# Batch 0's token scores on VectorE, y behind the first queries, first context blocks by thirds

## The chip, the core and the metric

One core of a Trainium2 chip runs the whole program in one launch. The metric is the device time of one execution in microseconds (us); all operands are float32. The engines are TensorE (PE, its weight loads PEld), VectorE (DVE), ScalarE (ACT), GpSimd (POOL) and SyncE (SP), which here only issues DMAs. Each engine works through its own queue in program order; the order is written out by hand in the source, and semaphores keep the data dependences.

## The reference

The inputs are 16 batches of 100 rows x (640 wide) and a context of 722 rows (384 wide), of which the last T = 4 are "tokens".

```python
query = x @ Wq;  keyt = enc @ Wk;  valt = enc @ Wv       # enc: 718 rows
hs = mha(query, keyt, valt)                              # 8 heads of 80
ca_q1 = einsum('btc,th->bch', ca, Wq_ca)[:, indices, :]  # ca: the 4 tokens
ca_hs1 = mha(ca_q1, x, x)
ca_hs2 = mha(ca_hs1 @ Wq, ca @ Wk_ca, ca @ Wv_ca)
out = (hs + ca_hs2) @ Wout + b_out + x
```

## The kernel before

**Context products.** Keys and values are made by a scheme that replaces the 18 block products of a 3 x 3 by 3 x 2 blocking by 15 products of sums of blocks. The context of a batch is cut into three thirds u of its 718 rows (240 columns each, transposed) and three chunks c of its 384 channels; `enc_sums` (L484) forms 13 sums or differences of these blocks on POOL (L505, 128x240 each), and `weight_sums` (L509) forms 12 differences of weight blocks on DVE (L529): 128x256 for the key weights `wk_sb`, 128x320 for the value weights `wv_sb`. `weight_sums(..., late)` takes the seven that leave the raw blocks alone (False), the five that overwrite them (True), or all. `Values` and `Keys` (L413, L456) go through a plan of 15 products in banks A to E; each product is copied (ACT, L410) or added (DVE, L408) into its place, and a bank cannot be used again before that.

**Start.** Five small matmuls run on zeros (`idle_ps`). Wk arrives transposed, by heads (`packed`, 96 KB each, even heads first, on the SP and ACT queues), and batch 0's context by single blocks (`load_first`, nine DMAs of 120 KB). `first_keys` (L595) turns Wk back on PE (`turn_back`, L587) and multiplies batch 0's keys directly, without the scheme: chunks 0 and 1 of the output with context channels c = 0 first, then three more `turn_back`s, then the rest (L619, 36 products in all). `last_keys` (L635) does the fifth chunk. In the trace one float32 product shows as two matmul records.

Behind it come, on DVE, the weight sums of `wk_sb`; on POOL two memsets and `enc_sums(enc)` of batch 0; on PE the tokens' keys `k_ps` (L1287), and from these, masked by heads on DVE (L1299), the products `m_ps` with Wq transposed (L1311), five of them, each copied by DVE (L1319). Three of the `wv_sb` sums stand on DVE behind each of the last four copies.

**Second attention.** `Second(b)` works out the token path. `keys(m)` (L765) places `m` into `m2` on POOL; `products` (L792) multiplies it with x to `y_ps` (L798) and sums `g` on DVE; `scores1` (L826) makes the 100 x 800 scores `e1` on POOL with four products (L833) and three additions (L840); `softmax1` (L844) finds their maximum by eight DVE steps of `Maximum` (L706) and subtracts it (L850); `exponentials1` (L852) is ACT's; `softmax2` (L855) multiplies by y to `z_ps` (L860).

For batch 0 the order is: `m_ps`, `last_keys`, `y_ps`, all five `queries` (L538), the tokens' values `va_ps`. POOL has batch 0's `scores1`, then `keys` and `enc_sums` for batch 1.

**Batch loop (L1366).** Per batch three groups of `scores` (L645, `s_ps`, copied by ACT at L681 and L687), their running maximum (`larger`, L1394 to L1396, and L1405), `z_ps`, the next batch's `y_ps`, then value products of this batch mixed with key products of the next (`vv.go`, `kk.go`, `both`). Between them stand `subtract` (L1384) and `exponential` (L1392) of the three score tiles, and at the end the products with the values (L1541, L1559). Batch 0 has an order of its own: three value and three key products, and the exponentials of its tokens between them, before `softmax2`. The last batch has no next keys; its value products follow `END_PLAN`, its third score tile is subtracted on POOL behind the first.

Of the kernel before, what the change touches and what calls it, by code (L numbers as in the profile page):

```python
# [10 lines left out]
ALU = mybir.AluOpType  # L11
# [4 lines left out]
NH, D = 8, 80  # L16
CAD, T = 384, 4
SK = 722 - T
P = 128
HC = H // P  # L20
CC = CAD // P

KT = SK // 3 + 1
# [124 lines left out]
def kernel(  # L148
# [144 lines left out]
    def load_first(queue, u, c):  # L293
        queue.dma_start(
            out=a_raw(enc, u, c),
            in_=enct[0][:, c, u * (KT - 1) : u * (KT - 1) + KT],
        )

    for h in range(0, NH, 2):
        (nc.scalar, nc.sync)[h // 2 % 2].dma_start(**packed(wkt_sb, wkt, h))  # L300
    load_first(nc.sync, 0, 0)
    load_first(nc.scalar, 1, 0)
    load_first(nc.sync, 2, 0)
    for h in range(1, NH, 2):
        (nc.scalar, nc.sync)[h // 2 % 2].dma_start(**packed(wkt_sb, wkt, h))
    nc.sync.dma_start(
        out=wkt_sb[:, 4], in_=wkt.rearrange("(h k) n -> h k n", h=NH)[:, 64:]
    )
    for c in range(1, CC):
        for u in range(3):  # L310
            load_first(nc.sync, u, c)
    tokens = pb_tile("tokens")
    beside = wide("beside")[:, : CC * (B * T + P)]
    cat_sb = beside[:, : CC * B * T].rearrange("p (c n) -> p c n", c=CC)
# [2 lines left out]
    nc.sync.dma_start(out=cat_sb, in_=cat.rearrange("p c b t -> p c (b t)"))  # L317
    nc.sync.dma_start(out=wkca_sb, in_=wkca.rearrange("(c p) n -> p c n", p=P))
    wqt_sb = wout_sb
    nc.sync.dma_start(out=wqt_sb, in_=wqt.rearrange("(c p) r -> p c r", p=P))  # L320
    nc.sync.dma_start(
        out=wv_sb[:, : 2 * CC].rearrange("p (c g) n -> p c (g n)", g=2),
        in_=wv.rearrange("(c p) n -> p c n", p=P),
    )
    xT = inp.tile([P, 2, HC, S], F32, tag="xT", name="xT_0", bufs=1)
    nc.sync.dma_start(out=xT, in_=xt[0:2].rearrange("b p c s -> p b c s"))
    halves = [t[:, u] for t in [scores_tile(f"wq_{i}") for i in range(NP)] for u in range(2)]
# [178 lines left out]
            begun = begun or first  # L506
        return begun

    def weight_sums(engine, w, late=None, part=slice(None)):  # L509
# [17 lines left out]
        for f, left, right in sums[part]:  # L527
            if late is None or late == (f in (5, 7, 13, 3, 14)):
                engine.tensor_tensor(at(f), left, right, ALU.subtract)  # L529
# [65 lines left out]
    def first_keys(enc):  # L595

        banks = {}
        copies = nc.scalar.copy, nc.vector.tensor_copy

        def begin(n, get):  # L600
            if get is pair:
                both = pair(f"kT_ps_0_{n}")
                banks[n] = [both[:, k] for k in range(2)]
            else:
                banks[n] = [get(f"kT_ps_0_{n}_{k}") for k in range(2)]

        for n in range(2):
            turn_back(n, nc.vector.tensor_copy)
            begin(n, pair)
        for c, chunks in ((0, (0, 1)), (0, (2, 3)), (1, range(4)), (2, range(4))):  # L610
            if len(banks) < 4 and 2 in chunks:
                for n in (2, 3, 4):
                    turn_back(n, copies[n % 2])
                begin(2, psum1)
                begin(3, psumk)
            for n in chunks:
                for bank, thirds in zip(banks[n], ((0, 1), (2,))):
                    for i, u in enumerate(thirds):
                        nc.tensor.matmul(  # L619
                            bank[:, i * KT : (i + 1) * KT],  # L620
                            wk_sb[:, 2 * c + n % 2, n // 2],
                            a_raw(enc, u, c),
                            start=(i == 0 and c == 0),
                            stop=(c == CC - 1),
                            skip_group_check=True,
                        )
        for n in banks:
            for bank, thirds in zip(banks[n], ((0, 1), (2,))):
                w = len(thirds)
                nc.scalar.copy(  # L630
                    kT[:, n, thirds[0] : thirds[0] + w],
                    bank[:, : w * KT].rearrange("p (u k) -> p u k", u=w),
                )
# [143 lines left out]
    class Second:  # L777
# [45 lines left out]
                ],  # L823
            )

        def scores1(self, behind=None, tokens=range(T)):  # L826
            b, g = self.b, self.g
            e = e1[:S].rearrange("p (h s) -> p h s", h=NH)
            for t in tokens:
                to = e if t == 0 else product_tile(f"e1_{b}_{t}")[:S].rearrange(  # L830
                    "p (h s) -> p h s", h=NH
                )
                first = nc.gpsimd.tensor_tensor(  # L833
                    to,
                    self.ca[:, t, :].unsqueeze(1).to_broadcast([S, NH, S]),
                    g[:, :, t].unsqueeze(2).to_broadcast([S, NH, S]),
                    ALU.mult,
                )
                if t:
                    nc.gpsimd.tensor_tensor(e, e, to, ALU.add)  # L840
                elif behind:
                    wait_for(first, behind)

# [418 lines left out]
    nc.gpsimd.memset(most[96:, :], LOW)  # L1262
    nc.gpsimd.memset(e1[96:, :], LOW)
    weight_sums(nc.vector, wk_sb, False)
    weight_sums(nc.vector, wk_sb, True)
    enc_sums(enc)

# [40 lines left out]
    for c in range(HC):  # L1308
        m_ps = psum(f"m_ps_{c}")
        for n, heads in enumerate(HEADS):  # L1310
            nc.tensor.matmul(  # L1311
                m_ps[:, heads[0] * B * T : (heads[-1] + 1) * B * T],
                wqt_sb[:, n, c * P : (c + 1) * P],
                k2T[n],
                start=(n == 0),
                stop=(n == HC - 1),
                skip_group_check=True,
            )
# [12 lines left out]
    second.copy()  # L1331
    second.scores1()
    keys(load_m(1))
    enc_sums(enc_next)
    tiles = queries_tiles(0)
    for n in range(HC):
        queries(0, xT, tiles, n)

    for e, lo in enumerate((64, 0)):
# [19 lines left out]
                    stop=(cc == CC - 1),  # L1359
                )  # L1360
    nc.scalar.copy(vaT.rearrange("p c n -> p (c n)"), va_ps[:, : HC * B * T])
    second.softmax1()

    xT_at = [None]
    last, late, second_next = None, False, Second(1, xT)
    for b in range(B):  # L1366
# [38 lines left out]
        nc.vector.tensor_tensor(most[:KN], st[0][:, 0], st[0][:, 1], ALU.max)  # L1405
# [24 lines left out]
        if b + 1 < B:  # L1430

            def both(n):
                vv.go(n)
                kk.go(n)
# [61 lines left out]
        else:  # L1496
# [132 lines left out]
```

## Time and profile before

| | us |
|---|---|
| median of 3 runs | 929.56 (929.08 to 931.22) |
| profiled execution | 928.27 |
| its span in the trace | 926.6 |
| PE busy | 913.8 (99%) |
| DVE, POOL, ACT busy | 659.0, 626.3, 376.1 |

The profiled execution's own time is 1.67 us longer than the span of its instructions. Times of the trace count from the start of the span. A row of the timeline merges equal instructions that follow each other: start, busy time, engine, line, operation, tiles, shapes, count, and in square brackets the idle time ahead and what ended it.

### The profile page before, as it was taken

The page shows a single profiled execution, that of the slowest core. Times are in us where ns is not written, and L with a number is a line of the kernel's source. Part 1 is how long each engine was busy: PE and PEld are TensorE (multiplying, and loading weights), DVE is VectorE, ACT ScalarE, POOL GpSimd, SP SyncE. Part 2 cuts the span into 40 slices and gives each one's busy share as a digit, 9 for nine tenths or more (in the row PEclk, how much of TensorE's full clock was granted, in tenths as well). Part 3 has the DMA queues.
Part 4 walks back from the last instruction along what each step waited for, and adds up shares of the span by engine and source line. Part 5 has one row for each costly group of instructions (what it writes and reads, how often), then busy time and mean ns, then how long its engine had stood idle before and what let it go on. Part 6 is the DMA issues. An engine that isn't in the chain of part 4 may idle for free.

```text
span 926.6 us, 26069 instructions
## 1 busy us (share of the span) xinstructions
PE 913.8 (99%) x11151; PEld 777.7 (84%) x11151; DVE 659.0 (71%) x1115; ACT 376.1 (41%) x654; POOL 626.3 (68%) x659
## 2 busy tenths in 40 slices
PE   9998999999999999999999999999999999999998
PEld 8976979888887989888798887988888888888865
DVE  2479796888729786685966759579792887828783
ACT  2343533435425354532434334344541444425351
POOL 9485788576955778477584766846796566955723
PEclk9999999999999999999999999999999999999999
DMA  8603262051401504141141402204140151401331
GB/s 288 211 13 83 64 131 73 6 141 34 109 11 34 141 6 109 44 118 25 40 103 43 131 12 65 78 15 133 43 109 10 34 138 37 110 11 45 86 84 32
DMA packets 68060, 69.50 MB, mean 75 GB/s; under 512 B 25192, under 2 KB 61352, under 8 KB 67944
## 3 DMA queue, kind: packets, MB, share of 16 engines
q1 hardware_dynamic: 67016, 66.97, 26.9%
q8 instruction: 88, 1.44, 0.7%
q10 hardware_dynamic: 464, 0.52, 0.2%
q0 software_dynamic: 464, 0.34, 0.2%
q14 instruction: 28, 0.23, 0.1%
HBM read 62.14 MB, written 8.94 MB: 77 GB/s over the span
## 4 chain that ended last, share of the span: by engine, by line
PE 95%; DVE 3%; issue 1%; ACT 1%; DMA 0%; ACTq 0%; DVEq 0%
PE s_ps L659 12%; PE v_psA L437 11%; PE v_psB L437 9%; PE k_psA L468 8%; PE a_ps L1559 7%; PE q_ps L542 7%; PE k_psB L468 6%; PE kT_ps L566 6%; PE r_ps L1541 4%; PE v_psC L437 4%; PE k_psC L468 3%; PE y_ps L798 2%; PE kT_ps L619 2%; PE o_psy L1127 2%; PE v_psD L437 2%; PE v_psE L437 2%
## 5 line engine op out<-in xcount | busy, mean ns | idle before, releaser
L833 POOL TENSOR_TENSOR e<-ca,g 100x800 f32<-100x800 f32 x64 | 97.8, 1540 | 95.6 <-DVE most L1396 77.8
L437 PE MATMUL v_psA<-wv_sb,enc 128*120 128x320 f32 x384 | 119.8, 434 | 4.1 <-DVE vs L408 3.1
L505 POOL TENSOR_TENSOR enc<-enc 128x240 f32<-128x240 f32 x144 | 110.7, 778 | 8.0
L840 POOL TENSOR_TENSOR e<-e,e 100x800 f32<-100x800 f32 x48 | 97.8, 2037 | 3.8
L437 PE MATMUL v_psB<-wv_sb,enc 128*120 128x320 f32 x320 | 99.2, 433 | 0.0
L659 PE MATMUL s_ps<-qp,kT 32*120 32x100 f32 x3072 | 97.5, 263 | 0.0
L659 PEld LDWEIGHTS s_ps<-qp,kT 32*120 32x120 f32 x3072 | 94.7, 180 | 1.9
L437 PEld LDWEIGHTS v_psA<-wv_sb,enc 128*120 128x120 f32 x384 | 68.9, 183 | 29.4 <-DVE vs L408 4.6
L1384 DVE TENSOR_TENSOR st<-st,over 120x1600 f32<-120x1600 f32 x47 | 90.5, 1926 | 0.0
L468 PE MATMUL k_psA<-enc,wk_sb 128*128 128x240 f32 x360 | 87.7, 367 | 0.2 <-DVE kT L408 0.2
L468 PEld LDWEIGHTS k_psA<-enc,wk_sb 128*128 128x128 f32 x360 | 68.4, 190 | 17.6 <-POOL e L833 0.7
L1396 DVE TENSOR_TENSOR most<-most,st 120x800 f32<-120x800 f32 x64 | 65.0, 1016 | 22.3 <-ACT st L681 20.6
L437 PEld LDWEIGHTS v_psB<-wv_sb,enc 128*120 128x120 f32 x320 | 58.7, 183 | 23.3
L1392 ACT ACTIVATE st<-st 120x1600 f32<-120x1600 f32 x48 | 73.9, 1540 | 4.1 <-DVE st L1384 3.6
L468 PE MATMUL k_psB<-enc,wk_sb 128*128 128x240 f32 x300 | 73.0, 366 | 0.0
L1405 DVE TENSOR_TENSOR most<-st 120x800 f32<-120x800 f32 x16 | 17.2, 1072 | 76.0 <-ACT st L687 76.0
L1559 PE MATMUL a_ps<-st,vs 120*64 120x100 f32 (+1 forms) x1536 | 69.5, 250 | 0.0
L542 PE MATMUL q_ps<-xT,wq_sb 128*128 128x200 f32 x400 | 69.0, 333 | 0.0
L1559 PEld LDWEIGHTS a_ps<-st,vs 120*64 120x64 f32 (+1 forms) x1536 | 66.4, 137 | 2.7 <-issue 2.7
L542 PEld LDWEIGHTS q_ps<-xT,wq_sb 128*128 128x128 f32 x400 | 67.9, 190 | 0.2
L410 ACT COPY vs<-v_psA 120x640 f32<-120x640 f32 x48 | 33.2, 693 | 85.2 <-PE v_psA L437 85.2
L687 ACT COPY st<-s_ps 120x800 f32<-120x800 f32 x64 | 49.7, 828 | 44.1 <-PE s_ps L659 44.1
(181 smaller groups left out, 1870.0 us busy)
## 6 DMA issues: line engine op xcount, KB each, us to landing
pb<-p_d SPq DMA_DIRECT2D x32, 400.0 KB
enc<-in_enct SPq DMA_DIRECT2D x30, 240.0 KB
enc<-in_enct SPq DMA_DIRECT2D x15, 360.0 KB
xT<-in_xt SPq DMA_DIRECT2D x8, 500.0 KB
rest<-in_enct SPq DMA_DIRECT2D x31, 120.0 KB
xn<-in_x SPq DMA_DIRECT2D x11, 320.0 KB
wide_d<-p_d SPq DMA_DIRECT2D x16, 200.0 KB
pb<-wide_d SPq DMA_DIRECT2D x16, 200.0 KB
```

The lines of the kernel that those rows point to most:

```text
L437: nc.tensor.matmul(at[0][j][:KN, : H // 2], a_form(self.enc, f)[:, j * KN : (j + 1) * KN], wv_sb[:, W_AT[f]], start=first, stop=last, skip ...
L468: nc.tensor.matmul(at[:, i * KT : (i + 1) * KT], wk_sb[:, W_AT[f], i], a_form(self.enc, f), start=(first and i == 0), stop=last, skip_grou ...
L505: first = nc.gpsimd.tensor_tensor(out, left, right, op)
L542: nc.tensor.matmul(q_ps[:, : 2 * S].rearrange("p (j s) -> p j s", j=2), wq_sb[:, c, n * P : (n + 1) * P], xT[:, :, c, :], start=(c == 0), ...
L566: nc.tensor.matmul(bank[:, i * KT : (i + 1) * KT], weights[c], a_raw(enc, u, c), start=(i == 0 and c == 0), stop=(c == CC - 1), skip_group ...
L659: nc.tensor.matmul(s_ps[bank][:n, 256 * a + lo : 256 * a + lo + rhs.shape[-1]], kT[rows, c, u, j * KN : (j + 1) * KN], rhs, start=bank not ...
L833: first = nc.gpsimd.tensor_tensor(to, self.ca[:, t, :].unsqueeze(1).to_broadcast([S, NH, S]), g[:, :, t].unsqueeze(2).to_broadcast([S, NH, ...
L840: nc.gpsimd.tensor_tensor(e, e, to, ALU.add)
L1384: return engine.tensor_tensor(st[i], st[i], top.over[:KN].unsqueeze(1).to_broadcast([KN, 2, ROWS]), ALU.subtract,)
L1392: nc.scalar.activation(st[i], st[i], AF.Exp, scale=SCALE)
L1396: most_now = nc.vector.tensor_tensor(most[:KN], most[:KN], st[i][:, u], ALU.max)
L1559: nc.tensor.matmul(wides[64 * e : 64 * e + 64, h // 2], slot(i, h, FIRST[e], 64), st[i // 2][: KEYS[i], i % 2, h * S : (h + 1) * S], start ...
```

## The change

- **First loads.** Batch 0's context comes in five DMAs in place of nine: third 0 whole (360 KB), third 1 as one block on ACT's queue and two on SP's, third 2 as two blocks and one. `first_keys` goes through the thirds in that order, all three channel chunks of a third together: chunks 0 and 1 with third 0, then with third 1, then the three `turn_back`s, chunks 2 and 3 with thirds 0 and 1, then all four with third 2.
- **Wv ahead of Wq transposed** in SP's queue, and all 12 `wv_sb` sums on DVE between the early and the late `wk_sb` sums.
- **y behind the first queries.** After `m_ps` PE does one of the five `queries`, then `y_ps`, then `last_keys`, then the other queries.
- **Batch 0's `scores1` on DVE** (seven operations of 100 x 800), with `softmax1` right behind; POOL goes from `keys` of batch 0 to `keys` and `enc_sums` of batch 1.
- **Batch 0 in the common order**: `exponentials1` behind the second group of scores, `softmax2` at once, then `both(3)`.
- **Last batch**: the additions of two value products (banks A and B) stand ahead of `subtract(0)`.

```diff
-    load_first(nc.sync, 0, 0)
-    load_first(nc.scalar, 1, 0)
-    load_first(nc.sync, 2, 0)
-    for h in range(1, NH, 2):
-        (nc.scalar, nc.sync)[h // 2 % 2].dma_start(**packed(wkt_sb, wkt, h))
+    load_heads(0)
+    load_first(nc.sync, 0, 0, 3)
+    load_first(nc.scalar, 1, 0, 1)
+    load_first(nc.sync, 1, 1, 3)
+    load_heads(1)
     nc.sync.dma_start(
         out=wkt_sb[:, 4], in_=wkt.rearrange("(h k) n -> h k n", h=NH)[:, 64:]
     )
-    for c in range(1, CC):
-        for u in range(3):
-            load_first(nc.sync, u, c)
+    load_first(nc.sync, 2, 0, 2)
+    load_first(nc.sync, 2, 2, 3)
...
-    nc.sync.dma_start(out=wqt_sb, in_=wqt.rearrange("(c p) r -> p c r", p=P))
     nc.sync.dma_start(
         out=wv_sb[:, : 2 * CC].rearrange("p (c g) n -> p c (g n)", g=2),
         in_=wv.rearrange("(c p) n -> p c n", p=P),
     )
+    nc.sync.dma_start(out=wqt_sb, in_=wqt.rearrange("(c p) r -> p c r", p=P))
...
-        for c, chunks in ((0, (0, 1)), (0, (2, 3)), (1, range(4)), (2, range(4))):
+        for u, chunks in (
+            (0, (0, 1)),
+            (1, (0, 1)),
+            (0, (2, 3)),
+            (1, (2, 3)),
+            (2, range(4)),
+        ):
...
-        def scores1(self, behind=None, tokens=range(T)):
+        def scores1(self, behind=None, tokens=range(T), engine=nc.gpsimd):
...
     weight_sums(nc.vector, wk_sb, False)
+    weight_sums(nc.vector, wv_sb)
     weight_sums(nc.vector, wk_sb, True)
     enc_sums(enc)
...
         nc.sync.dma_start(out=m_d[c], in_=m_sb[c])
-        if c:
-            weight_sums(nc.vector, wv_sb, part=slice(3 * c - 3, 3 * c))
     nc.sync.dma_start(out=wvca_sb, in_=wvca.rearrange("(c p) n -> p c n", p=P))
     second = Second(0, xT, ca_0)
     keys(load_m(0))
-    last_keys(0, enc)
+    tiles = queries_tiles(0)
+    queries(0, xT, tiles, 0)
     second.products()
     second.copy()
-    second.scores1()
+    second.scores1(engine=nc.vector)
+    second.softmax1()
     keys(load_m(1))
     enc_sums(enc_next)
-    tiles = queries_tiles(0)
-    for n in range(HC):
+    last_keys(0, enc)
+    for n in range(1, HC):
         queries(0, xT, tiles, n)
...
     nc.scalar.copy(vaT.rearrange("p c n -> p (c n)"), va_ps[:, : HC * B * T])
-    second.softmax1()
...
         larger(1)
+        if b == 0:
+            now.exponentials1()
         st.append(scores(b, 2, tiles))
...
-        if b == 0:
-            seen = larger(2)
-            vv.go(2)
-            kk.go(2)
-            now.exponentials1()
-            vv.go(1)
-            kk.go(1)
         now.softmax2()
...
-        if b:
-            seen = larger(2)
+        seen = larger(2)
...
-            both(3 if b else 0)
+            both(3)
...
             top.go(1)
             top.go()
+            vv.go(2)
             less = subtract(0)
             exponential(0)
             wait_for(subtract(2, nc.gpsimd), less)
-            vv.go(5)
+            vv.go(3)
             last.put()
```

More of the change, by code (lines that the diff above doesn't have):

```diff
@@ L291, with load_first, load_heads @@
     enc = enc_tile("enc_0"), rest_tile("rest_0")
-    def load_first(queue, u, c):
+    def load_first(queue, u, lo, hi):
+        to = a_raw(enc, u, lo) if hi == lo + 1 else enc[0][:, A_RAW[u, lo] :][:, : hi - lo]
         queue.dma_start(
-            out=a_raw(enc, u, c),
-            in_=enct[0][:, c, u * (KT - 1) : u * (KT - 1) + KT],
-        )
-    for h in range(0, NH, 2):
-        (nc.scalar, nc.sync)[h // 2 % 2].dma_start(**packed(wkt_sb, wkt, h))
-    load_first(nc.sync, 0, 0)
-    load_first(nc.scalar, 1, 0)
-    load_first(nc.sync, 2, 0)
-    for h in range(1, NH, 2):
-        (nc.scalar, nc.sync)[h // 2 % 2].dma_start(**packed(wkt_sb, wkt, h))
+            out=to,
+            in_=enct[0][:, slice(lo, hi) if hi > lo + 1 else lo, u * (KT - 1) : u * (KT - 1) + KT],
+        )
+    def load_heads(u):
+        for h in range(u, NH, 2):
+            (nc.scalar, nc.sync)[h // 2 % 2].dma_start(**packed(wkt_sb, wkt, h))
+    load_heads(0)
[3 more added lines that the diff above has]
+    load_heads(1)
     nc.sync.dma_start(
@@ L507, in enc_sums, with weight_sums @@
         return begun
-    def weight_sums(engine, w, late=None, part=slice(None)):
+    def weight_sums(engine, w, late=None):
         at = lambda f: w[:, W_AT[f]]
@@ L526, in weight_sums @@
         )
-        for f, left, right in sums[part]:
+        for f, left, right in sums:
             if late is None or late == (f in (5, 7, 13, 3, 14)):
@@ L616, in first_keys @@
             for n in chunks:
[L617 to L626, printed above, removed]
+                for c in range(CC):
+                    nc.tensor.matmul(
+                        banks[n][u // 2][:, u % 2 * KT : (u % 2 + 1) * KT],
+                        wk_sb[:, 2 * c + n % 2, n // 2],
+                        a_raw(enc, u, c),
+                        start=(u != 1 and c == 0),
+                        stop=(c == CC - 1),
+                        skip_group_check=True,
+                    )
         for n in banks:
@@ L832, in scores1 @@
                 )
-                first = nc.gpsimd.tensor_tensor(
+                first = engine.tensor_tensor(
                     to,
@@ L839, in scores1 @@
                 if t:
-                    nc.gpsimd.tensor_tensor(e, e, to, ALU.add)
+                    engine.tensor_tensor(e, e, to, ALU.add)
                 elif behind:
```

## The prediction, on record before the changed kernel ran

> **What bounds the kernel now.** I read the page first, for the engine that carries the chain, then PE's own waits, because only they can be won. The span, and the chain that ended last by engines:
>
> ```profile
> span 926.6 us, 26069 instructions
> ...
> PE 95%; DVE 3%; issue 1%; ACT 1%; DMA 0%; ACTq 0%; DVEq 0%
> ```
>
> PE carries 95% of the chain. The change takes no product away, so its worth is the idle time of PE that goes, less what comes. The view of PE's waits (who, for whom, us in total, times, longest) shows how little there is:
>
> ```profile
> PE v_psA L437 <- DVE vs L408: 3.1, 2, 1.8
> ...
> PE k_psE L468 <- DVE vs L408: 0.9, 1, 0.9
> PE k_psD L468 <- ACT vs L410: 0.7, 1, 0.7
> ...
> PE k_psA L468 <- DVE kT L408: 0.2, 1, 0.2
> ```
>
> One of the two 3.1 us waits is in the last batch (1.31, below). The rest lies in batch 0's loop, with one more that has its row below (0.97 at 56.95): 1.8 + 0.9 + 0.7 + 0.2 + 1.0 = 4.6 us. That, the 1.31 and what the start holds is all that can be won. PE's timeline of the start:
>
> ```profile
> 4.71 1.51 PE L587 MATMUL w_ps<-e,kT 128*128 128x128 f32 x6 [1.06 <-DMA kT<-in_wkt]
> 6.23 1.17 PE L619 MATMUL kT_ps<-enc,wk_sb 128*128 128x240 f32 x2
> ...
> 7.99 1.81 PE L619 MATMUL kT_ps<-enc,wk_sb 128*128 128x240 f32 x4
> 9.59 0.65 PE L619 MATMUL kT_ps<-rest,wk_sb 128*128 128x240 f32 x2
> ...
> 10.49 1.15 PE L587 MATMUL w_ps<-e,kT 128*128 128x128 f32 x9
> ...
> 13.68 6.24 PE L619 MATMUL kT_ps<-enc,wk_sb 128*128 128x240 f32 x30
> ...
> 24.21 1.97 PE L1287 MATMUL k_ps<-beside,tokens 128*64 128x64 f32 x60 [0.24 <-ACT kT L630]
> 26.64 6.91 PE L1311 MATMUL m_ps<-wq,wout_sb 128*128 128x128 f32 x50 [0.46 <-DVE wq L1299]
> ```
>
> Two things are to be seen. From 6.23 PE does not stop, so the loads cost nothing after that. And its pace changes: from 7.99 to 9.59 four records take 1.60 (0.40 each), from 13.68 thirty take 6.24 (0.20 to 0.21 each), though the granted clock reads 1.00. The six products between 6.23 and 10.49 run at half pace for most of the way.
>
> **The change, part by part.**
>
> *First context blocks by thirds.* The first product now waits for a whole third (360 KB) where 120 KB did. What has been moved, by stretch (columns: length, PE busy, PEld, DVE, ACT, POOL, clock, DMA share, GB/s):
>
> ```profile
> 0.00:2.50 2.50, 1.36 (x6) 1.36 (x7) 0.17 (x1) 0.00 (x0) 1.71 (x10) 1.00 0.21 55
> 2.50:5.00 2.50, 1.44 (x8) 1.17 (x7) 0.00 (x0) 1.16 (x1) 2.19 (x4) 1.00 1.00 259
> 5.00:7.50 2.50, 2.49 (x9) 1.97 (x8) 1.11 (x2) 0.12 (x1) 2.50 (x6) 1.00 0.82 204
> ```
>
> Up to that third SP has 2 x 96 + 360 = 552 KB, and ACT's queue beside it 4 x 96 + 120 = 504 KB, together 1,081 kB. By 5.0 us 2.5 x (55 + 259) = 785 kB are there; at 204 per us the rest comes by 6.45, and the signal of it later; if the other queues take more, by 7.5, when 1,295 kB have moved. I take 7.4: 1.2 us late (0.2 to 1.4). Nothing covers this; PE has no other work.
>
> The three `turn_back`s come behind 12 products, not 6. If PE's half pace lasts as long from its new start as from the old (to about 9.8, 3.57 us), 4.5 of the 12 run at 0.80 (two records) and 7.5 at 0.405: 7.4 + 3.57 + 3.05 = 14.0 where it was 10.49. Call this shift X = 3.5; bounds 2.4 (third 0 there in time) and 4.5 (the pause prolongs the half pace). The keys end only 1.2 later, since the products are the same; the 0.24 ahead of `k_ps` goes, as the first-third banks are copied early.
>
> *Wv's sums on DVE.* This is the term that decides. DVE is in order: 7 early `wk_sb` sums, 12 `wv_sb` sums, 5 late ones, and only then the masks (L1299) for which `m_ps` waits. Beside them POOL runs its 13 `enc_sums`. DVE and POOL rows:
>
> ```profile
> 12.01 4.28 DVE L529 TENSOR_TENSOR wk_sb<-wk_sb 128x256 f32<-128x256 f32 x8
> ...
> 13.69 2.59 DVE L529 TENSOR_TENSOR wk_sb<-wk_sb 128x256 f32<-128x256 f32 x3
> ...
> 24.00 1.56 DVE L529 TENSOR_TENSOR wk_sb<-wk_sb 128x256 f32<-128x256 f32 x4 [7.71 <-PE kT_ps L619]
> ...
> 30.23 1.44 DVE L529 TENSOR_TENSOR wv_sb<-wv_sb 128x320 f32<-128x320 f32 x3
> ```
>
> ```profile
> 13.53 0.80 POOL L505 TENSOR_TENSOR enc<-enc 128x240 f32<-128x240 f32 x1
> ...
> 59.90 5.75 DVE L1396 TENSOR_TENSOR most<-most,st 120x800 f32<-120x800 f32 x4 [0.53 <-DVE most L1405]
> ...
> 158.14 2.55 DVE L961 TENSOR_TENSOR wout_t<-wout_sb,wout_t 128x640 f32<-128x640 f32 x2
> ```
>
> The first row's eight are five and the second row's three. The five pass from 12.01 to 13.69, 0.34 each; as soon as POOL begins at 13.53 a sum takes about 0.85 (2.59 for the three); alone again, at 24.00, 0.39. [...] L961 (1.27 for 640 columns) and L1396 (1.43 for 800), both beside L505, both fit about 0.57 for POOL's turn plus 0.001 for each column, and so does 256 columns at 0.84. So a `wv_sb` sum of 320 columns costs 0.91 beside POOL, and alone between 0.39 and 0.48 (last row); I take 0.40, as rows of one group overlap.
>
> Now the sum. DVE starts at 12.01 + 3.5 = 15.5. POOL's second memset waits for the `turn_back`s too, so its sums start 0.95 later, at 16.5 (13.53 before). Until then 3 sums at 0.34; then 4 at 0.84 and 9 at 0.91 beside POOL's 13, 11.6 us, to 28.1; then 3 at 0.40 and 5 at 0.39, 3.15, to 31.2; the first mask 0.4. `m_ps` starts at 31.6 where it started at 26.64: **+5.0** (X plus 1.46; 3.9 to 6.0 over X's bounds). PE meanwhile has finished `k_ps` at about 26.2 + 1.0 = 27.2 and idles 4.4. The same sums cost nothing before: they stood between copies that kept ahead of `m_ps`. Wq transposed lands one Wv (983 kB) later, far ahead of 31.6, and Wv, by its place in the queue, ahead of DVE's eighth sum.
>
> *Scores on DVE, batch 0 in the common order.* Now POOL ends `scores1` late and DVE's maximum starts at 50.71:
>
> ```profile
> 50.71 1.01 DVE L722 STREAM_TRANSPOSE turned<-e 128x800 f32<-128x800 f32 x1 [12.26 <-POOL e L840]
> ...
> 57.11 1.36 DVE L850 TENSOR_TENSOR e<-e,over 100x800 f32<-100x800 f32 x1
> ```
>
> PE's rows up to the scores and behind them:
>
> ```profile
> 33.38 1.38 PE L566 MATMUL kT_ps<-enc,wk 128*128 128x240 f32 x6
> ...
> 37.03 1.12 PE L798 MATMUL y_ps<-m,xT 128*100 128x96 f32 x10
> 37.99 8.65 PE L542 MATMUL q_ps<-xT,wq_sb 128*128 128x200 f32 x50
> ...
> 48.64 1.10 PE L659 MATMUL s_ps<-qp,kT 32*120 32x100 f32 x32
> ...
> 56.95 1.34 PE L437 MATMUL v_psA<-wv_sb,enc 128*120 128x320 f32 x4 [0.97 <-ACT st L687]
> ```
>
> DVE's chain ends at 58.47, 9.8 us behind the start of the scores on PE (48.64) and 2.5 behind their end (56.95 - 0.97 = 55.98), and holds up the running maximum and every addition behind it.
>
> After: last keys (37.03 - 33.38 = 3.65), four of five queries (8.65 x 4/5 = 6.9) and values (from 46.64 to 48.64, 2.0) lie between `y_ps` and the scores, so `g` is there 12.2 us ahead of them (12.6 less 0.4 for its own way). Seven operations, the first two alone (1.0), five beside POOL's `enc_sums` of batch 1 at the 1.43 of L1396, are 9.1; maximum and subtraction last 7.3 to 7.8 (50.71 to 58.47). They end 4.7 behind the scores' start instead of 9.8. Next late are the exponentials, on ACT behind the second group's copies:
>
> ```profile
> 53.70 1.68 ACT L681 COPY st<-s_ps 120x400 f32<-120x400 f32 x4 [0.79 <-PE s_ps L659]
> ...
> 61.48 0.87 ACT L853 ACTIVATE e<-e 100x800 f32<-100x800 f32 x1
> ```
>
> 53.70 + 1.68 + 0.87 = 56.25 against the scores' end at 55.98, and a step to get there: `z_ps` waits 0.35. The rest of the batch then stands as the later ones, in which PE's waits show nothing. So **-4.6 + 0.35 = -4.25** (-4.6 to -2.5).
>
> *y behind the first queries.* POOL's `keys` follow each copy of `m_ps`; for the last one there is now a query's time on PE (8.65 for five, 37.99: 1.7) in place of `last_keys`' 3.65, and no `wv_sb` sums stand ahead of it on DVE any more. I take 0; at most 0.3, an estimate.
>
> *Last batch.* The wait, and what follows it on the other engines:
>
> ```profile
> 897.83 1.34 PE L437 MATMUL v_psA<-wv_sb,enc 128*120 128x320 f32 x4 [1.31 <-DVE vs L408]
> ...
> 904.38 1.24 PE L437 MATMUL v_psA<-wv_sb,enc 128*120 128x320 f32 x4
> ```
>
> ```profile
> 895.21 1.83 DVE L1384 TENSOR_TENSOR st<-st,over 120x1600 f32<-120x1600 f32 x1
> 896.95 0.82 DVE L408 TENSOR_TENSOR vs<-v_psA,vs 120x640 f32<-120x640 f32 x1
> ...
> 897.18 3.59 POOL L1384 TENSOR_TENSOR st<-st,over 120x1600 f32<-120x1600 f32 x1 [7.74 <-DVE st L1384]
> ...
> 901.67 1.54 ACT L1392 ACTIVATE st<-st 120x1600 f32<-120x1600 f32 x1
> 903.11 0.68 ACT L410 COPY vs<-v_psA 120x640 f32<-120x640 f32 x1
> ```
>
> With both additions first (two at 0.82 and their gaps) the 1.31 goes, but `subtract(0)` ends at 895.21 + 1.65 + 1.83 = 898.7, POOL's subtraction behind it runs 3.59 to 902.3, the third exponential on ACT starts at 902.4 instead of 901.67, and the copy of bank A behind that ends at 904.6. The bank's next product, at 904.38 now, needs it. The gain is handed back: **+0.2** (-0.3 to +0.6).
>
> Sum against the profiled execution (928.27, of which 1.67 outside the span): 5.0 - 4.25 + 0.2 = +0.95, so 929.2. That execution lies 1.3 below the median, which moves by as much: 929.56 + 0.95 = **930.5**.
>
> **The rivals.**
>
> *Forecast: DVE's queue holds `m_ps` for about as much as batch 0 gives back.* Own range 929.1 to 932.1, from X's bounds and the other terms' ends. 0.46.
>
> *Slower: PE loses its pace in the new pause.* For: half pace at the start, behind an idle PE; 3.6 us of it from 6.23, half of which is lost, 1.8. Against: behind 1.31 idle the four records at 897.83 take 1.34, against 1.24 without a pause at 904.38, so the pace is kept there. A pause of 4.4 is longer than any that the waits show (1.8). It decides from the point where the pause is long enough; then `m_ps` runs its first part at half pace: +1.8 to +3.4 (half of the whole 6.91), most likely 2.4, 932.9. 0.26.
>
> [...]
>
> *Faster: the sums slip past POOL.* If POOL gave way, 19 sums of 0.34 and 0.40 would end by 23, ahead of the keys; `m_ps` would then follow the keys, 1.0 late, and the sum is 1.0 - 4.25 + 0.2 = -3.05: 926.5. Against it three views (L529, L961, L1396); for it only that POOL's start and Wv's landing shift in ways that I bound from rows of another order. 0.20.
>
> *The reordering does not do what it says:* the scores on DVE meet POOL for longer, at 1.9 each, the maximum is late by 3 more, and half of batch 0's stalls stay: +2.1, 932.6. 0.08.
>
> **How the numbers follow.** A measurement of this kernel tells 0.2% (1.9 us) from no change. Below 927.7 lie the third case and a little of the first: 0.22. Above 931.4 lie the second, the fourth and the upper tail of the first (0.04): 0.37. Between: 0.41. The range goes from the third case, 926.2, to the second with a large X, 933.8.
>
> **What would show it.** Right: PE idles 3 to 6 us ahead of `m_ps`, released by DVE's L1299; `wv_sb` sums take about 0.9 while POOL's sums run; the idle rows between 56 and 76 are gone, and 0.35 stands at `z_ps`; 897.83's wait is smaller and a wait for ACT has come a few products later. Half pace would show as `m_ps` well over 6.91. Wrong: `wv_sb` sums of 0.4 beside POOL, `m_ps` less than 2 late, or waits left in batch 0.

## The result, and the profile after

The changed kernel takes 931.63 us (median of 20 runs, 929.01 to 933.11), the kernel before beside it 929.26 (20 runs, 928.41 to 931.22). The ratio is 1.0021, 95% interval 1.0013 to 1.0028: slower by 0.2%, 2.4 us at the medians. The profiled execution of after took 931.78, span 930.1.

The page of after, its span and its chain by engines, then the view of PE's waits (engine, tile, line, who ended the wait, us in total, times, longest):

```profile
span 930.1 us, 26065 instructions
...
PE 96%; DVE 2%; DMA 1%; issue 0%; POOL 0%; ACT 0%; SPq 0%; DVEq 0%
```

```profile
PE m_ps L1319 <- DVE wq L1307: 4.6, 1, 4.6
PE kT_ps L626 <- DMA enc<-in_enct: 1.5, 1, 1.5
...
PE z_ps L867 <- issue: 1.0, 2, 0.5
...
PE v_psA L439 <- ACT vs L412: 0.7, 1, 0.7
PE v_psC L439 <- DVE vs L410: 0.4, 1, 0.4
PE z_ps L867 <- ACT e L860: 0.2, 1, 0.2
```

Batch 0's waits are gone but for 0.21 at `z_ps`. In the last batch 0.36 and 0.66 stand where 1.31 was (the two waits for L410 and L412). At the start two waits are new or much longer: 1.5 for the first third, 4.6 ahead of `m_ps`. Line numbers have moved by 2 to 8 (`m_ps` L1311 is L1319, the masks L1299 are L1307, the weight sums L529 are L531). PE's timeline of the start and the scores:

```profile
7.58 5.14 PE L626 MATMUL kT_ps<-enc,wk_sb 128*128 128x240 f32 x12 [1.48 <-DMA enc<-in_enct]
12.50 1.01 PE L626 MATMUL kT_ps<-rest,wk_sb 128*128 128x240 f32 x2
13.30 1.07 PE L626 MATMUL kT_ps<-enc,wk_sb 128*128 128x240 f32 x4
14.21 0.57 PE L626 MATMUL kT_ps<-rest,wk_sb 128*128 128x240 f32 x2
...
15.42 0.82 PE L589 MATMUL w_ps<-e,kT 128*128 128x128 f32 x6
...
26.40 1.97 PE L1295 MATMUL k_ps<-beside,tokens 128*64 128x64 f32 x60
32.97 8.98 PE L1319 MATMUL m_ps<-wq,wout_sb 128*128 128x128 f32 x50 [4.60 <-DVE wq L1307]
...
57.04 1.10 PE L666 MATMUL s_ps<-qp,kT 32*120 32x100 f32 x32
```

The first rows show half pace (two records in 1.01; 0.40 a record, against 0.20 later) until about 13.5; the three `turn_back`s come at 15.42 instead of 10.49. `m_ps` starts at 32.97 instead of 26.64 and takes 8.98 instead of 6.91. The reason for its length is in the view of stretches of one microsecond (length; PE, PEld, DVE, ACT, POOL busy; granted clock; DMA share; GB/s):

```profile
29.00:30.00 1.00, 0.00 (x0) 0.00 (x0) 1.00 (x3) 1.00 (x5) 0.56 (x1) 1.00 0.69 233
30.00:31.00 1.00, 0.00 (x0) 0.00 (x0) 1.00 (x3) 0.92 (x4) 0.00 (x0) 0.77 0.13 43
...
36.00:37.00 1.00, 1.00 (x6) 1.00 (x6) 0.62 (x1) 0.00 (x0) 0.29 (x1) 0.50 0.00 0
37.00:38.00 1.00, 1.00 (x8) 1.00 (x8) 0.00 (x0) 0.00 (x0) 0.00 (x0) 0.81 0.52 199
```

0.77 in one stretch means 0.46 us of it at 0.50, 0.81 means 0.38. The clock is at 0.50 from 30.54 to 37.38, which covers the end of the pause and the first 4.4 us of `m_ps`. DVE's queue ahead of it, and POOL's beside it:

```profile
16.95 3.94 DVE L531 TENSOR_TENSOR wk_sb<-wk_sb 128x256 f32<-128x256 f32 x7
20.81 9.90 DVE L531 TENSOR_TENSOR wv_sb<-wv_sb 128x320 f32<-128x320 f32 x12
30.64 2.07 DVE L531 TENSOR_TENSOR wk_sb<-wk_sb 128x256 f32<-128x256 f32 x5
32.62 1.21 DVE L1307 TENSOR_TENSOR wq<-k_ps,hmask 128x128 f32<-128x128 f32 x5
```

```profile
18.00 0.93 POOL L507 TENSOR_TENSOR enc<-enc 128x240 f32<-128x240 f32 x1
...
26.93 2.63 POOL L507 TENSOR_TENSOR enc<-enc 128x240 f32<-128x240 f32 x3
```

DVE does not rest from 16.95 to the masks. POOL's sums fill 18.0 to 29.6, nearly all of the twelve `wv_sb` sums (0.83 each).

### The profile page after: what moved, and what is told of

The parts are those of the page before. It is cut to its first block, busy times and chain, and to the rows that moved or that the text cites. A ratio compares the mean times of both kernels' runs of the same rounds, so it can differ in the third digit from the quotient of the medians.

```text
span 930.1 us, 26065 instructions
## 1 busy us (share of the span) xinstructions
PE 916.3 (99%) x11151; PEld 781.3 (84%) x11151; DVE 672.0 (72%) x1122; ACT 375.5 (40%) x654; POOL 616.1 (66%) x652
## 4 chain that ended last, share of the span: by engine, by line
PE 96%; DVE 2%; DMA 1%; issue 0%; POOL 0%; ACT 0%; SPq 0%; DVEq 0%
PE s_ps L666 12%; PE v_psA L439 11%; PE v_psB L439 9%; PE k_psA L470 8%; PE a_ps L1561 7%; PE q_ps L544 7%; PE k_psB L470 7%; PE kT_ps L568 6%; PE r_ps L1543 4%; PE v_psC L439 3%; PE k_psC L470 3%; PE y_ps L805 2%; PE v_psD L439 2%; PE v_psE L439 2%; PE o_psy L1134 2%; PE k_psE L470 1%
## 5 line engine op out<-in xcount | busy, mean ns | idle before, releaser
L840 POOL TENSOR_TENSOR e<-ca,g 100x800 f32<-100x800 f32 x60 | 91.7, 1539 | 102.1 <-DVE most L1403 87.9
L847 POOL TENSOR_TENSOR e<-e,e 100x800 f32<-100x800 f32 x45 | 92.1, 2047 | 3.5
L412 ACT COPY vs<-v_psA 120x640 f32<-120x640 f32 x48 | 33.2, 693 | 84.4 <-PE v_psA L439 84.3
```

The lines of the kernel that those rows point to most:

```text
L840: first = engine.tensor_tensor(to, self.ca[:, t, :].unsqueeze(1).to_broadcast([S, NH, S]), g[:, :, t].unsqueeze(2).to_broadcast([S, NH, S] ...
L847: engine.tensor_tensor(e, e, to, ALU.add)
```

## The experiments

The disputed points are which part costs what, why `m_ps` is late, and whether the clock is part of the price. All edits are to the changed kernel, except where batch 0's part stands alone.

**Wv's sums back behind `m_ps`'s copies.**

```diff
-    weight_sums(nc.vector, wv_sb)
...
+        if c:
+            weight_sums(nc.vector, wv_sb, part=slice(3 * c - 3, 3 * c))
```

> The changed kernel with one thing undone: the 12 wv sums stand again in threes behind the last four copies of m_ps; everything else stays changed. If DVE's queue is what holds m_ps: the wait ahead of m_ps falls from 4.60 to about 0.5, the granted clock stays at 1.00 and m_ps lasts 6.9 in place of 8.98; the copies now lag behind m_ps, so y_ps waits 1 to 1.6 for POOL's keys; sum about -4.1 - 2.1 + 1.3, some 5 us less than the changed kernel where that lost its pace, 926 to 928 us, faster than before by 1 to 3. If the wait belongs to the later end of the keys (thirds) or to late data instead: it stays over 2 us and the time within 2 us of the changed kernel's.

Measured: 925.45 us (925.29 to 927.17), ratio to before 0.9964 (0.9951 to 0.9976). From PE's timeline of this kernel:

```profile
28.09 6.91 PE L1318 MATMUL m_ps<-wq,wout_sb 128*128 128x128 f32 x50 [0.86 <-DVE wq L1306]
...
38.34 0.41 PE L805 MATMUL y_ps<-m,xT 128*100 128x96 f32 x2 [0.85 <-POOL m L777]
```

The pause and the lost clock are gone together, and the thirds remain with a start of `m_ps` 1.45 later than before the change. A new wait of 0.85 stands at `y_ps`: the last copies of `m_ps` now stand behind Wv's sums on DVE, and there is only one query to hide that.

**POOL's sums of batch 0 held until DVE's last weight sum.** (`weight_sums` also returns its last operation.)

```diff
-    weight_sums(nc.vector, wk_sb, True)
-    enc_sums(enc)
+    done = weight_sums(nc.vector, wk_sb, True)
+    wait_for(enc_sums(enc), done)
```

> The changed kernel, with POOL's 13 sums of batch 0 held until DVE has done its last weight sum; DVE's order is unchanged. If DVE and POOL take turns: the 12 wv sums take about 0.40 each (0.83 in the changed kernel), DVE ends its early and wv sums before the keys are done, and the wait ahead of m_ps falls from 4.60 to about 0.5 with the clock at 1.00; POOL's keys for y then come up to 2 late. If the position in DVE's queue alone is to blame (or Wv's landing): the sums keep 0.8 each or wait for Wv, and the wait ahead of m_ps stays over 3.

Measured: 925.64 (925.08 to 926.25), ratio 0.9959 (0.9945 to 0.9974). DVE's and PE's timelines:

```profile
19.91 5.16 DVE L531 TENSOR_TENSOR wv_sb<-wv_sb 128x320 f32<-128x320 f32 x12
```

```profile
29.44 6.91 PE L1320 MATMUL m_ps<-wq,wout_sb 128*128 128x128 f32 x50 [0.46 <-DVE wq L1308]
```

The same twelve sums, at the same place in the queue, take 5.16 instead of 9.90 when POOL is still: 0.43 each instead of 0.83. That shows that POOL's work is what slows DVE's. POOL's sums are slower beside DVE's as well: 0.77 to 0.95 each in the changed kernel, against 0.69 or 0.70 in the kernel before while DVE stood idle. But the two do not simply take turns: a DVE sum alone (0.43) and a POOL sum alone (0.69) are 1.12, and beside each other one of each passes in 0.83 to 0.89.

**Context by single blocks again.** (The loads and the loop of `first_keys` as before the change; Wv's sums stay early.)

```diff
-    load_first(nc.sync, 0, 0, 3)
-    load_first(nc.scalar, 1, 0, 1)
-    load_first(nc.sync, 1, 1, 3)
+    load_first(nc.sync, 0, 0)
+    load_first(nc.scalar, 1, 0)
+    load_first(nc.sync, 2, 0)
...
-        for u, chunks in (
...
+        for c, chunks in ((0, (0, 1)), (0, (2, 3)), (1, range(4)), (2, range(4))):
```

> The changed kernel with batch 0's context loaded and multiplied again by single blocks, channel chunk by channel chunk. If the turn_backs' place sets when DVE can begin: PE's wait of 1.48 for the context goes, the first DVE sum starts at about 12.0 (16.95 in the changed kernel), m_ps starts at about 28.1 (32.97) behind a wait of about 1.9, too short for the clock, which stays at 1.00; the time is 5 us below the changed kernel's slower runs, about 926.5, 2.5 to 3 below before. If the thirds cost only the 1.2 us of their wait: 930 us or more and a wait ahead of m_ps still over 3.

Measured: 925.55 (925.0 to 928.15), ratio 0.9966 (0.9954 to 0.9977). DVE and PE:

```profile
18.10 8.42 DVE L529 TENSOR_TENSOR wv_sb<-wv_sb 128x320 f32<-128x320 f32 x12 [4.40 <-DMA wv_sb<-in_wv]
```

```profile
28.77 8.48 PE L1312 MATMUL m_ps<-wq,wout_sb 128*128 128x128 f32 x50 [3.34 <-DVE wq L1300]
```

The time is as good as with Wv's sums back, but not by the steps that I had written: DVE got to Wv's sums 4.4 us before Wv was there, and the pause of 3.34 cost the clock in the profiled execution (`m_ps` 8.48). That execution took 926.96. Its mean clock is 0.998, as in two more of the seven (926.96 to 928.15); four read 0.999 and took 925.0 to 925.55, so the median stands for executions that lost less of the clock. `m_ps` starts 4.2 earlier than in the changed kernel.

**The pause filled with 22 products on zeros.**

```diff
+    for _ in range(22):
+        nc.tensor.matmul(k2_ps[:, 384:], idle, idle, start=True, stop=True)
```

> The changed kernel with 22 extra products on zeros in the pause ahead of m_ps (4.7 us of PE work at full pace, results unused). If the pause itself takes PE's pace away: the granted clock stays at 1.00, m_ps lasts 6.9 in place of 8.98, m_ps starts where it did or up to 0.5 later, and the runs lie at 929 to 931, about 1 below the changed kernel's median. If m_ps is slow for another reason (its operands or the masks arriving one by one): it keeps about 9 and the time is that of the changed kernel or more.

Measured: 929.51 (927.38 to 931.96), ratio 1.0002 (0.9992 to 1.0012), so 0.19% or 1.8 us under the changed kernel.

```profile
32.72 6.91 PE L1321 MATMUL m_ps<-wq,wout_sb 128*128 128x128 f32 x50 [0.46 <-DVE wq L1309]
```

`m_ps` takes 6.91 again. The added products take away PE's idle time and leave the other engines' work as it was, so the 2.07 on `m_ps` is the clock's price, and idle PE time alone brought it. That `m_ps` starts where it did (32.72 against 32.97) is chance: in this execution the `turn_back`s came 1.2 earlier (14.21), and the added products, which write to the same tile as `k_ps`, held the masks for 0.85:

```profile
32.38 1.22 DVE L1309 TENSOR_TENSOR wq<-k_ps,hmask 128x128 f32<-128x128 f32 x5 [0.85 <-PE k_ps L1303]
```

**Batch 0's part alone.** (Against the kernel before; also batch 0's `larger(2)`, `both(3)` and exponentials as changed, nothing else.)

```diff
-    last_keys(0, enc)
+    tiles = queries_tiles(0)
+    queries(0, xT, tiles, 0)
     second.products()
     second.copy()
-    second.scores1()
+    second.scores1(engine=nc.vector)
+    second.softmax1()
     keys(load_m(1))
     enc_sums(enc_next)
-    tiles = queries_tiles(0)
-    for n in range(HC):
+    last_keys(0, enc)
+    for n in range(1, HC):
```

> The kernel before with batch 0's part of the change alone: the tokens' scores and softmax 1 on VectorE, y behind the first queries, batch 0 in the common order. The context comes by single blocks, Wv's sums stand behind m_ps's copies, the last batch reads as before. Theory (the gain is batch 0's stalls, and it is whole without the other parts): the first products and m_ps start as before, about 26.6 us; y_ps waits about 0.85 for POOL, as it did with the sums back in their old place; no waits from 56 to 80 us but about 0.2 at z_ps; the time is 4.25 - 0.85 = 3.4 us under the kernel before, about 926. Rival (the thirds or the last batch carry part of the gain that the run with the sums back showed): at most 2 us under, 927.5 or more.

Measured: 924.64 (924.14 to 924.94), ratio 0.9953 (0.994 to 0.9967). `m_ps` starts at 27.02, `y_ps` waits 0.85, and of waits behind the scores only 0.21 at `z_ps` and the last batch's are left. The part brings 4.3 us, more than the 3.4 that I expected (see the next section).

With the runs above this makes a table of two factors, batch 0's part being in all four. Ratio to before:

| | Wv's sums behind `m_ps` | Wv's sums early |
|---|---|---|
| single blocks | 0.9953 | 0.9966 |
| thirds | 0.9964 | 1.0021 |

(The last batch's edit is in all but the first, and Wv stands ahead of Wq transposed in all but the first.) Alone the thirds cost 0.11% and the early sums 0.13%, about 1 us each; by the intervals (about 0.13% on each ratio) neither is clear of noise. Together they cost 0.68%, 6.3 us, which is. They do not add: in the profiles with the thirds DVE's queue starts 4.9 us later and all its Wv sums meet POOL's. With single blocks POOL had five of its sums done, at 0.69 each, before Wv landed.

**Single blocks, and POOL's sums held until Wv's last.** (The loads and `first_keys` as in the run with single blocks, and:)

```diff
-    weight_sums(nc.vector, wv_sb)
+    done = weight_sums(nc.vector, wv_sb)
     weight_sums(nc.vector, wk_sb, True)
-    enc_sums(enc)
+    wait_for(enc_sums(enc), done)
```

> The changed kernel with the context by single blocks again and POOL's sums of batch 0 held until VectorE's last sum of Wv. Theory (turns of VectorE and POOL and the thirds are the two losses): no wait at the first product of the keys; VectorE waits for Wv until about 18.1 us, then 12 sums at 0.43 to about 23.3 and five at 0.34 to about 25.2, so that m_ps waits about 0.5 as before the change and starts at 26.6 to 27; no pause over 1 us, clock 1.00 throughout; the time is 4 us under the kernel before, about 925.0, and 0.5 under the runs with one part undone. Rival (POOL's held sums come late for the keys of batch 1): a new wait of about 1 to 3 us ahead of the first Keys sums or of y_ps, 926 to 928.

Measured: 924.61 (923.58 to 926.5), ratio 0.9956 (0.9943 to 0.9968). It is no better than batch 0's part alone. The profile:

```profile
28.84 6.91 PE L1313 MATMUL m_ps<-wq,wout_sb 128*128 128x128 f32 x50 [2.23 <-DVE wq L1301]
```

`m_ps` waited 2.23, not 0.5: Wv landed at 19.74, and POOL's held sums then met the five late `wk_sb` sums, 3.77 for five:

```profile
24.82 3.77 DVE L529 TENSOR_TENSOR wk_sb<-wk_sb 128x256 f32<-128x256 f32 x5
```

The pause of 2.23 left the clock at 1.00 in this execution. One of the five reads a mean clock of 0.997, and it is the slowest, 926.5.

**The last batch's edit undone** (one execution, read in its profile).

```diff
-            vv.go(2)
             less = subtract(0)
...
-            vv.go(3)
+            vv.go(5)
```

> The changed kernel with the last batch's order as before the change (one addition ahead of the subtraction, five behind). Read in the profile only, from the first product of bank A after the pause to a_ps. Theory (the gain is handed back): a wait of 1.3 us for VectorE stands at v_psA again, the two short waits of 0.4 and 0.7 at v_psC and v_psA go, and the stretch is 19.85 us where the changed kernel has 20.07. Rival (the edit is worth its 1.3 us, and the stretch of the changed kernel was long for another reason): the stretch is 21 us or more. The start is unchanged, m_ps at about 33 us.

Measured from the first product of bank A in its last stretch to `a_ps`: 896.80 to 916.56, 19.76 us, with a wait of 1.22 for DVE; the changed kernel's 896.65 to 916.72 is 20.07. The gain is handed back with 0.3 on top. Over all profiles the stretch from the last batch's first `o_ps` to `a_ps` is 25.60 to 26.48 in the seven with the edit and 25.40 to 25.97 in the six without it, so the edit shows no gain; whether it costs anything is not clear of the spread.

**Scores on POOL, all else as with Wv's sums back.**

```diff
-    second.scores1(engine=nc.vector)
+    second.scores1()
```

> The kernel with Wv's sums back in their old place, and with the tokens' scores on POOL again; softmax 1, y and the order of batch 0 stay as changed. Theory (the scores' engine is what takes batch 0's stalls away): POOL's seven operations take about 2.3 us each or more and end some 5 us later than VectorE's, VectorE's maximum starts at about 52 or later, and PE waits again between 56 and 80 us, 2 to 4 us in all; the time is 927.5 to 929.5 against 925.45 with them on VectorE. Rival (the order, not the engine, takes the stalls away): the waits stay under 0.7 us in all, time 925 to 926.

Measured: 929.23 (927.9 to 931.17), ratio 1.0003 (0.9994 to 1.0012), against 0.9964 with the scores on DVE. PE's waits and DVE's timeline:

```profile
PE kT_ps L626 <- DMA enc<-in_enct: 2.5, 1, 2.5
PE z_ps L867 <- ACT e L860: 1.7, 1, 1.7
...
PE k_psE L470 <- DVE vs L410: 0.9, 1, 0.9
```

```profile
52.61 1.01 DVE L729 STREAM_TRANSPOSE turned<-e 128x800 f32<-128x800 f32 x1 [12.28 <-POOL e L847]
```

In this kernel the scores' first product stands at 52.32, 1.14 later than with DVE (the first third came later in this execution); the first `o_ps` of the last batch stands at 889.60 against 883.95, 5.65 later. The difference, 4.5, is not all the engine's. Batch 0 alone, from the first product of its scores to that of batch 1, lasts 53.48 us in the kernel before, 51.34 here, and 47.82 or 47.83 in all eleven profiles with the scores on DVE. So the engine is worth 3.5, inside the 2 to 4 that I expected, and the order without the engine 2.1. The other 1.0 lies in later batches, whose code is the same, and where executions of equal code differ by up to 1.2. The later start of the scores (52.32 against 48.64 in the kernel before) takes the 2.1 back.

**Wv's sums split: six early, two each behind three copies.** (Batch 0's part alone, with Wv ahead of Wq transposed.)

```diff
     weight_sums(nc.vector, wk_sb, False)
+    weight_sums(nc.vector, wv_sb, part=slice(6))
...
-        if c:
-            weight_sums(nc.vector, wv_sb, part=slice(3 * c - 3, 3 * c))
+        if c < 3:
+            weight_sums(nc.vector, wv_sb, part=slice(6 + 2 * c, 6 + 2 * c + 2))
```

> Batch 0's part alone as in the run before, with Wv's sums dealt differently: six behind the weights' own eight, where VectorE stands idle for 7 us (17.2 to 24.4), and two each behind the first three copies of m_ps. Wv is loaded ahead of Wq transposed. Theory (the 0.85 ahead of y_ps is the last m_ps copies standing behind Wv's sums on VectorE): the six sums take 0.4 to 0.9 each and end by 24.5, m_ps still waits about 0.5, the wait at y_ps goes; 0.85 under batch 0's part alone, about 923.8. Rival (Wv lands too late, or POOL's turns stretch the six past 24.5): m_ps waits 1 to 2.5 us, and the time is 924.6 to 926.

Measured: 923.10 (922.42 to 924.16), ratio 0.9945 (0.9931 to 0.9958), the lowest median of all, though its interval overlaps those of the two runs above at 0.9953 and 0.9956. DVE:

```profile
19.41 5.31 DVE L529 TENSOR_TENSOR wv_sb<-wv_sb 128x320 f32<-128x320 f32 x6 [2.95 <-DMA wv_sb<-in_wv]
```

Six sums beside POOL (0.89 each) just fit ahead of the keys' end; `m_ps` waits 0.46 and the wait at `y_ps` is gone.

**A pause alone.** Batch 0's part alone, and the first mask run 8 or 16 times more.

```diff
+        for _ in range(1 if n else 9):
             nc.vector.tensor_tensor(
```

> Batch 0's part alone, with a pause put ahead of m_ps and nothing else: the first mask's multiplication on VectorE is run eight more times with the same result, about 0.25 us each, so that m_ps waits about 2.5 us instead of 0.47. Theory (a pause costs the clock only from some length between 2.2 and 3.3 us): clock 1.00 behind it, m_ps 6.91, time 924.6 + 2.0 = 926.6. Rival (the clock went in the changed kernel for another reason than the pause's length, the load of the other engines for instance): the same here, told apart by the next run.

> As the run with the pause of about 2.5 us, with sixteen more multiplications: m_ps waits about 4.5 us. Theory: the clock reads 0.50 from about 3 us into the pause until some 6.5 us later, m_ps takes 8.5 to 9.0 instead of 6.91, time 924.6 + 4.0 + 1.6 to 2.1 = 930.2 to 930.7. Rival (not the pause's length): clock 1.00, m_ps 6.91, time 928.6.

Measured: 927.87 (926.77 to 928.67), ratio 0.999 (0.9981 to 0.9999), and 931.62 (930.37 to 932.28), ratio 1.003 (1.0018 to 1.0041). One more mask took 0.32, not 0.25, so the pauses came out longer than meant. `m_ps` with the shorter one, then with the longer:

```profile
28.51 8.52 PE L1312 MATMUL m_ps<-wq,wout_sb 128*128 128x128 f32 x50 [3.06 <-DVE wq L1300]
```

```profile
31.38 9.17 PE L1312 MATMUL m_ps<-wq,wout_sb 128*128 128x128 f32 x50 [5.66 <-DVE wq L1300]
```

Both cost the clock: 1.61 and 2.26 on `m_ps`. For the shorter one I had expected 1.00. So idle time is enough as a cause. In the profiles the pause of 2.23 cost nothing and all from 3.06 up did. With one profile for each length, that gives no fixed limit (see the last section). The stretches of the shorter pause in which the clock goes and comes back:

```profile
28.00:29.00 1.00, 0.49 (x3) 0.49 (x4) 0.97 (x5) 1.00 (x4) 0.00 (x0) 0.84 1.09 360
...
32.00:33.00 1.00, 1.00 (x9) 1.00 (x8) 0.04 (x1) 0.00 (x0) 0.29 (x1) 0.95 0.11 42
```

## Why the prediction was right or wrong

The forecast was 930.5 and the time is 931.63, inside the forecast's own range. But its mechanism was not the whole: the rival "PE loses its pace in the new pause" came true as well. The sum against the profiled executions was +0.95 and came out at 3.5 (the spans). By its terms, from the timelines:

| term | predicted | measured |
|---|---|---|
| start of `m_ps` | +5.0 | +6.33 (26.64 to 32.97) |
| length of `m_ps` | 0 (rival +1.8 to +3.4) | +2.07 (6.91 to 8.98) |
| batch 0's loop, to the scores of batch 1 | -4.25 | -5.66 (53.48 to 47.82) |
| from there to the last batch's first `o_ps` | 0 | +0.79 (785.36 to 786.15) |
| last batch | +0.2 | +0.22 |

What is left, -0.25, lies behind `a_ps`. The number is partly luck. `m_ps` starts 1.3 later and takes 2.1 longer than the forecast had it, batch 0 gives back 1.4 more, and the median moved by only 2.4 where the profiled executions differ by 3.5: that of before lies 1.0 under the median of its 20 runs, that of after at it.

*Thirds: a term that was mis-sized.* The first product waited 1.48 (predicted 1.2). X, the shift of the `turn_back`s, is 4.93, not 3.5, and above my bound of 4.5. The step that failed is that half pace lasts as long from its new start as from the old (3.57). It lasted from 7.58 to about 13.5, 5.9 us. I had counted from the first product of the keys, 6.23; but PE had been busy without a gap since 4.71, so half pace had lasted 5.05 already in the kernel before. With 5.05 the same working gives X = 4.3, an estimate. I had also read the clock as 1.00 there. The trace's own record of the clock only begins with the rise to full, at 9.76 before and 13.49 after, and the views fill the time ahead of it with 1.00. In both, that first entry stands where the pace of the records goes from 0.40 to 0.20, and the pace changes so in all thirteen profiles. So the half pace at the start is the clock. From the start of unbroken work on PE the rise came after 3.4 to 6.1 us, with blocks as with thirds, so X differs between executions too: the `turn_back`s stand at 9.74 to 10.99 in the seven profiles with single blocks and at 14.21 to 16.18 in the six with thirds, 4.9 apart on average.

So the keys end 2.2 later (`k_ps` 24.21 to 26.40), not 1.0. In the six profiles with thirds the first wait was 0.58, 1.45, 1.48, 2.22, 2.31 and 2.47; with single blocks it was at most 0.18. The wait of one execution is no measure of this load.

*Wv's sums: right in mechanism and in sum.* X plus 1.46 with the measured X is 6.39, and `m_ps` is 6.33 late. Two sizes were off by 0.5 each and cancel: the seven early sums took 3.94 (predicted 4.38), the twelve of Wv 9.90 (predicted 9 x 0.91 + 3 x 0.40 = 9.39), as POOL stood beside nearly all of the twelve. A sum took 0.83 beside POOL (predicted 0.91) and 0.43 alone (0.40). The 0.91 was an estimate from rows of the kernel before beside POOL's sums (about 0.85 for 256 columns, 1.27 for 640, 1.43 for 800); no run shows its split into a turn of POOL's of 0.57 and 0.001 for each column. PE paused 4.60 (predicted 4.4). Holding POOL back and moving the sums both take the pause away. The rival in which the sums slip past POOL falls.

*Loss of pace: I held it the less likely, by a row too short to say so.* The row against it was a pause of 1.31. In the profiles the pauses of 3.06 and more cost the clock, and a pause of 4.4 is well over that. The case for it, half pace at the start, was the right row to read, as that is the clock as well. The price of 2.4 was near the 2.07 measured.

*Batch 0: right in mechanism, 1.4 too small.* `g` is there 12.1 ahead of the scores (predicted 12.2), the seven operations take 9.6 (9.1), and VectorE's subtraction ends at 62.00, 4.96 behind the scores' start at 57.04 (predicted 4.7). `z_ps` waits 0.21 for the exponentials (0.35), and no other wait stands in the batch.

```profile
61.01 0.99 DVE L857 TENSOR_TENSOR e<-e,over 100x800 f32<-100x800 f32 x1
```

The idle time that went is 4.60 - 0.21 = 4.39, near the 4.25. What I left out is that a wait costs more than its idle time. The view of stretches for batch 0's loop, in the kernel before, in the changed kernel, and with the scores left on POOL (length, PE busy and records, then the other columns as above):

```profile
48.64:102.12 53.48, 48.89 (x647) 40.19 (x645) 47.40 (x77) 21.75 (x35) 39.59 (x42) 1.00 0.23 63
57.04:104.86 47.82, 47.61 (x647) 40.62 (x645) 43.18 (x73) 21.76 (x35) 26.30 (x26) 1.00 0.25 67
52.32:103.66 51.34, 48.41 (x647) 40.15 (x646) 47.27 (x77) 21.47 (x35) 36.61 (x41) 1.00 0.23 64
```

The same 647 records keep PE busy 1.28 longer in the kernel before, about 0.26 for each of its five waits. The rows show why: the busy time of a row of value products reaches about 0.16 into the next row, which at a wait it can't, and the first row behind a wait lasts 1.34 instead of 1.24. With the scores left on POOL 3.5 of the 5.66 is lost, and on VectorE they take 1.28 to 1.38 each, not 1.9, so the reordering rival falls. The 0.79 behind batch 0 lies within the spread between executions: in five profiles with the same code from batch 0's scores to the last batch's `o_ps` that stretch lasts 832.77 to 833.97, and the changed kernel's has the longest. *y behind the first queries* cost 0 in the changed kernel, as taken; with Wv's sums behind the copies it costs 0.85, outside my bound of 0.3, because that bound counted on those sums being gone.

*Last batch: right.* The copy of bank A on ACT became the late step, as worked out:

```profile
908.03 1.34 PE L439 MATMUL v_psA<-wv_sb,enc 128*120 128x320 f32 x4 [0.66 <-ACT vs L412]
```

What stays open: why the first third's landing differs by 1.9 us between executions, and why batches 3, 8 and 11 differ by up to 1.0 us between executions of the same code.

## What to carry to other kernels

Work that is moved ahead of a step on an in-order engine is free only as long as the queue behind it ends before the slowest other condition of that step; sum the queue with the durations that hold beside the other engine, where the two slow each other (here 0.83 for a `wv_sb` sum beside POOL's sums), and not with those of the engine alone (0.43). Two edits that each eat the same slack (a later start, a longer queue) do not add: here some 1 us each, not clear of noise, became 6.3 together, so try them apart. And price a pause of PE twice: its length, and the products behind it at half clock once it is longer than the longest pause that the profile shows without harm (here 2.23 left `m_ps` at 6.91, and 3.06 made it 8.52, in one profile each). A shorter wait also costs more than its idle time, here about 0.26 us each, as products no longer overlap.

## What the runs showed of the hardware

Behind the long pauses the lost clock had one of two lengths. By the stretches in which the clock reads between 0.50 and 1.00 it was at 0.50 for 3.42 us behind the pauses of 3.06 (28.68 to 32.10) and 3.34 (28.72 to 32.14), and for 6.84 and 6.82 behind 4.60 (30.54 to 37.38) and 5.66 (29.34 to 36.16); the run with the last batch's edit undone, with a pause of 4.61, has 6.82 as well. It fell between 2.1 and 3.6 us behind the last product of `k_ps`, at no fixed distance, and at the end of the program about 5 us behind the last product of all, in the kernel before (5.1) and in the changed one (5.0). So a pause of 2.23 that left the clock alone in one execution need not do so in the next. At the start full pace came 3.4 to 6.1 us after PE began to work without a gap: 5.05 in the kernel before (4.71 to 9.76), 5.91 in the changed one (7.58 to 13.49).

The mean clock of each execution fits the two lengths: of the changed kernel's 20 runs twelve read 0.998 (median 930.59) and eight 0.996 (median 932.08), and 3.4 and 6.8 us at half in 930 would be that. It proves little by itself, as the kernel before reads 0.996 to 1.000 too without a pause of PE over 1.8 us in its profile. That profile shows no loss inside the span, so where its other executions lose the clock stays open.
